# Eleven output products beside the last subtiles, folding of queries beside stage 2's products, and stage 2's bias on VectorE

## The chip, the cores and the metric

The kernel runs on one core of a Trainium2 chip. That core has five engines that run side by side: TensorE (PE in the profile; PEld is its weight load), VectorE (DVE), ScalarE (ACT), GpSimd (POOL) and SyncE (SP, which here only issues transfers). They share the on-chip memory SBUF; TensorE writes into the eight banks of PSUM, from which VectorE and ScalarE read. Transfers to and from the chip's main memory run on 16 DMA engines, and are issued from the queues of SP, ACT and POOL. Each engine works through its own instructions in a fixed order. The metric is device time in microseconds (us) from one launch.

## The reference

All is float32. Two cross-attentions follow each other over 4 x 1024 tokens of width 1024, each with a context of 64 rows per batch:

```python
# layer 0: 32 query heads of 32, 8 key/value heads
q, k, v = x @ Wq + bq, ctx @ Wk + bk, ctx @ Wv + bv
attn = softmax(q k^T / sqrt(32) + mask)           # per head, over 64 keys
h = (attn v) @ Wo + bo + x
x = layernorm(h, eps 1e-6) * gamma + beta
# layer 1: 16 heads of 64
a = layernorm(ctx) ; Q, K, V = x @ Wq.T, a @ Wk.T, a @ Wv.T
out = softmax(Q K^T / 8, masked) V @ Wo.T
y = x + tanh(gate) * out
```

## The kernel before, in words

Tokens come in 32 subtiles of 128 (t = 0 to 31), four blocks of eight, or 16 pairs. Large products are done in blocks of a two by two split, with seven products of blocks in place of eight (`products`, seven steps named X, V and W after the PSUM bank that each sums in). One step is four matmuls of 128 x 128 by 128 x 512, which the trace shows as eight records of L446, and one add of the bank to the row tile on VectorE (L455). The left operand's sums (`left_out`, L429 to L432) and the right operand's (`right_sums`, L183 to L186) are VectorE's too.

Stage 1 computes queries (L576) and layer 0's attention. For each subtile `mix` emits: two fronts (`front`, TensorE's scores L680 and VectorE's mask add L684), maxima (L691), subtraction of the maxima (L694), exponentials on ScalarE (whole in L706, or for `alone` heads one by one with their sum, L698), sums (L711), division (L715), then a transpose of the probabilities (`flip`; from subtile 19 on by TensorE, L407, with copies L410 or L414), the product with the values (`values`, L759) and a store of the result (L765). Between these, `other()` draws steps from one generator, `other_work`: the queries of later blocks, then the folding of layer 1's query weights into the keys, then the first steps of the output product of pair 0.

Folding of queries (`folded_queries`, eight chunks of four steps) multiplies K transposed by a chunk of Wq: per step four matmuls of 64 rows by 256 columns (L897, eight records), two evictions on ScalarE (L903), and after every second step a store of 1 MB on POOL's queue (L909). It also loads a chunk of wq1T on SP (L884). Eight steps go ahead of subtile 24 (`FOLD_AHEAD`), the other 24 and the first four product steps (`FIRST`) are shared out over the last eight subtiles. The weight wo is loaded in 16 parts on SP (L147).

Stage 2 is the output product: after the last three steps of pair 0, pairs 1 to 15 go through `project`, seven products with L455's adds, and between them steps of `fill`: the closing of the pair before (layer norm, L292 to L309, and its store L1053) and, for pairs 1 to 8, the folding of values into wo1 (`folded_values`, two steps `keys` of matmuls L924, evictions L929 and stores on SP L933). Rows of x come on SP (L954); the bias bo is added to them ahead of time on GpSimd (L958), for pair 0 on VectorE afterwards (L1095). Stage 3 is layer 1's attention with the folded weights. PSUM has four single banks (`wx`) and two double ones (`big`).

The kernel is written with a planner. It takes the program's order as priority and plans each engine's order from modelled times: an instruction whose inputs are ready in the model can go ahead of one that waits. `keep_in_program_order` exempts an instruction from that. Buffers come from pools with a number of slots per tag (`wpool`, tag "wb", has seven); a tile whose slot is in use waits for its release.

Of the kernel before, what the change touches and what calls it, by code (L numbers as in the profile page):

```python
# [19 lines left out]
B = 4  # L20
# [51 lines left out]
def tile_two_cross_attentions(  # L72
# [27 lines left out]
    def sub_ap(t):  # L100
        return slice(t * P, (t + 1) * P)
# [6 lines left out]
    ps_wx = ctx.enter_context(tc.tile_pool(name="ps_wx", bufs=4, space=bass.MemoryType.PSUM))  # L108
    ps_big = ctx.enter_context(tc.tile_pool(name="ps_big", bufs=2, space=bass.MemoryType.PSUM))

# [6 lines left out]
    def wx():  # L117
        return ps_wx.tile([P, 512], F32, tag="wx", name="wx")

# [21 lines left out]
    def block_of(w, i, j, tag, name, turned=False):  # L141
        t = new_block(tag, name)
        cols = slice(j * HW, (j + 1) * HW)
        if turned == "heads":
            rows = w.rearrange("(c g i e d) o -> c i e d g o", c=2, g=4, i=2, e=2)
            for a in range(NQ):
                nc.sync.dma_start(  # L147
                    out=t[a * Q : (a + 1) * Q], in_=rows[a // 2, a % 2, i][:, :, cols]
                )
        elif turned:  # L150
            rows = w.rearrange("(a k j) o -> a j k o", a=NQ, j=Q)
            for a in range(NQ):
                nc.sync.dma_start(
                    out=t[a * Q : (a + 1) * Q], in_=rows[a, :, i * HK : (i + 1) * HK, cols]
                )
        else:
            nc.sync.dma_start(
                out=t, in_=w[i * HW : (i + 1) * HW, cols].rearrange("(k p) o -> p k o", p=P)
            )
        return t  # L160
# [274 lines left out]
    def products(a, w, r, bias=None, tail=None):  # L435
# [6 lines left out]
        def product(name, s, m, first, last):  # L442
            if first:
                banks[name] = wx()
            for k in range(HK):
                nc.tensor.matmul(  # L446
                    banks[name], a[s][:, k, :], w[m][:, k, :],
                    start=first and k == 0, stop=last and k == HK - 1, skip_group_check=True,
                )
# [28 lines left out]
        ]  # L478
        return [lambda o=o: step(*o) for o in order]

    def project(a, w, r, fill, bias=None, tail=None):

        share = -(-len(fill) // 7)
        for step in products(a, w, r, bias, tail):
            step()
            for _ in range(min(share, len(fill))):
                fill.pop(0)()
# [150 lines left out]
    def by_turning(t):  # L638


        return t < NSUB - SUB - 5
# [12 lines left out]
    def attend0(t):  # L654
# [13 lines left out]
        alone = BY_HEAD if by_turning(t) else (4, 0) if t >= NSUB - SUB else (0, 0)  # L668
# [218 lines left out]
    def folded_queries(kT, wT, k):  # L887
# [3 lines left out]
        def heads(cc):  # L891
            banks = [wx(), wx()]
# [47 lines left out]
    def load_o(pair, pool, tag="o2"):  # L940
        o = pool.tile([P, KC, 2 * P], F32, tag=tag, name=f"o2_{pair}")
        load = nc.sync.dma_start(out=o, in_=oTd[pair])
        if pair < 2:
            tc.keep_in_program_order(load)
        return o

    def load_outputs(pair):
        o = load_o(pair, o2pool) if pair > 1 else second if pair else load_o(0, early)
        r = []
        for u in range(2):  # L950
            t = pair * 2 + u
            ru = (rpool.tile([P, H], F32, tag="r", name=f"r_{t}") if pair
                  else early.tile([P, H], F32, tag="r", name=f"r_{t}", bufs=2))
            load = nc.sync.dma_start(out=ru, in_=x[sub_ap(t), :])  # L954
            if not pair:
                tc.keep_in_program_order(load)
            if pair:
                nc.gpsimd.tensor_tensor(ru, ru, bo_sb, ALU.add)  # L958
            r.append(ru)
        return o, r  # L960

    def other_work(rows):

        nonlocal fold, early, bo_sb, w_o, first, first_rows, second
# [12 lines left out]
        queries_cm.close()  # L977
        fold = open_pool(fold_cm, "fold", 1)

        early = open_pool(early_cm, "early", 1)  # L980
        kT = fold.tile([P, KC, B * S], F32, tag="kvT", name="kT")
        nc.sync.dma_start(out=kT, in_=kTd)
        wT = turned_chunk(0)
        w_o, w_o_loads = right_loads(wo0, "wa", "wo0", "heads")
        bo_sb = constant(bo0.partition_broadcast(P), [P, H], "bo", F32, fold)
        for k in range(KC):
            ahead = turned_chunk(k + 1) if k + 1 < KC else None
            for step in folded_queries(kT, wT, k):
                step()
                yield  # L990
            wT = ahead
            if k in (1, 2, 3, 4):
                w_o_loads[k - 1]()
            if k == 5:
                run(right_sums(w_o))
                o, first_rows = load_outputs(0)
                a = left_out(o, early, "0_0")
        second = load_o(1, wpool, "wb")

        def tail():  # L1000
            nonlocal ahead_a
            ahead_a = left_out(second, early, "0_1")


        first = products(a, w_o, first_rows, None, tail)
        for _ in range(FIRST):
            first.pop(0)()
            yield

    fold_cm, early_cm = ExitStack(), ExitStack()  # L1010
    fold = early = bo_sb = w_o = first = first_rows = second = ahead_a = ahead_r = None
    FIRST = 4
# [3 lines left out]
    AHEAD, FOLD_AHEAD = 4, 8  # L1016
# [11 lines left out]
    n = 4 * KC - FOLD_AHEAD + FIRST  # L1028
    for i in range(SUB):
        mix(last + i, (i + 1) * n // SUB - i * n // SUB)  # L1030
# [17 lines left out]
    vT = fold.tile([P, KC, B * S], F32, tag="kvT", name="vT")  # L1048
# [20 lines left out]
    def turn_x1(pair, xq, pool=None, tag="xT"):  # L1069
# [15 lines left out]
    first.pop(0)()  # L1085
    flip(0)
    flip(1)
    first.pop(0)()
    values()
    open_stage()  # L1090
    _, ahead_r = load_outputs(1)
    run(first)

    fill = [
        lambda u=u: nc.vector.tensor_tensor(first_rows[u], first_rows[u], bo_sb, ALU.add) for u in range(2)  # L1095
    ]
    fill += close_rows(0, first_rows)
    for pair in range(1, NPAIR):
        r, a = ahead_r, ahead_a
        if pair + 1 < NPAIR:  # L1100
            ahead_o, ahead_r = load_outputs(pair + 1)
        if pair <= KC:
            ahead_w = chunk(wo1, pair, "wo1") if pair < KC else None
            fill += folded_values(vT, wch, pair - 1)
            wch = ahead_w
        if pair == KC + 2:
            w_a, w_a_sums = right_weight(ad[0], "wb", "a0", True)
        if pair in (NPAIR - 3, NPAIR - 2):
            fill += w_a_sums[0:2] if pair == NPAIR - 3 else w_a_sums[2:4]
        if pair == 3:  # L1110
            early_cm.close()
            xTpool = open_pool(last_cm, "x1T", 1)
            lxpool = open_pool(last_cm, "leftx", 1)
            xqpool = open_pool(last_cm, "x1q", 1)
        if pair == NPAIR - 4:
            xq = load_x1(1)
# [10 lines left out]
        project(a, w_o, r, fill, tail=tail)  # L1127
        fill = close_rows(pair, r)
# [112 lines left out]
    fold_cm.close()  # L1241

# [54 lines left out]
```

## Time and profile before

| | |
|---|---|
| Median of 3 runs | 1914.9 us (1913.46 to 1915.07) |
| The profiled execution | 1915.11 us, of which the span of its instructions is 1913.3 us |
| TensorE / VectorE / ScalarE / GpSimd busy | 1868.9 / 1292.1 / 427.9 / 179.1 us |
| Mean granted TensorE clock | 0.995 |
| Last subtiles (24 to 31), VectorE from its first to its last part | 598.9 to 705.4 us |
| Stage 2, pairs 1 to 15 | from about 720 to 1130 us |
| GpSimd's bias adds (L958) | 30, 2625 ns each |

A row of a timeline or chain reads: start, duration, engine and line, operation, out<-in by the program's names, shapes and a count; in brackets the idle time of the engine before it and what ended it. A row of windows gives for each engine its busy time in the window and the number of instructions, then TensorE's granted clock, the mean busy share of the DMA engines, and GB/s. A busy TensorE may still run below its peak, since matmuls are pipelined and the clock can be throttled.

### The profile page before, as it was taken

Reading aid. Unit: us, or ns where it says so; the run is one execution under the profiler, and the core shown is the slowest. Engines: PE = TensorE matmul, PEld = TensorE weight load, DVE = VectorE, ACT = ScalarE, POOL = GpSimd, SP = SyncE. Lnnn points to the kernel's source line nnn. Section 1 sums busy time; section 2 is a strip of 40 time slices with the busy share of each in tenths; the row PEclk is TensorE's granted clock in tenths of the full one; section 3 lists DMA queues with packets and bytes.
Section 4 is the critical chain, followed back from the end, with each engine's and each line's share of the span. In section 5 each row is a group of like instructions: output and inputs, shape, how many; then the busy total and the mean of one; then the engine's idle time right before and its main releaser. Section 6 shows DMA issues by size and latency. Waiting matters only on the chain.

```text
span 1913.3 us, 17522 instructions
## 1 busy us (share of the span) xinstructions
PE 1868.9 (98%) x6096; PEld 880.0 (46%) x6096; DVE 1292.1 (68%) x1582; ACT 427.9 (22%) x1396; POOL 179.1 (9%) x212
## 2 busy tenths in 40 slices
PE   8999999999998899999999999999999999999999
PEld 7744444444455653343344444444444444444444
DVE  3425589789878985575568778557665766576653
ACT  1101575666536751212100001000000000000000
POOL 0016011111100103121113100000000000000000
PEclk9999999999999899999999999999999999999999
DMA  8996599899878966567473363466656565657421
GB/s 276 184 222 192 158 253 247 253 252 261 252 186 275 302 234 207 188 207 238 164 218 138 121 141 90 110 165 158 150 143 165 150 158 143 165 142 165 121 88 44
DMA packets 220745, 350.54 MB, mean 183 GB/s; under 512 B 26992, under 2 KB 146160, under 8 KB 215664
## 3 DMA queue, kind: packets, MB, share of 16 engines
q1 hardware_dynamic: 152896, 242.44, 45.8%
q0 software_dynamic: 15216, 60.83, 10.5%
q10 hardware_dynamic: 52544, 46.14, 8.8%
q8 instruction: 48, 0.79, 0.2%
q14 instruction: 41, 0.34, 0.1%
HBM read 207.53 MB, written 141.82 MB: 183 GB/s over the span
## 4 chain that ended last, share of the span: by engine, by line
PE 82%; DVE 8%; DMA 5%; issue 2%; ACT 2%; POOL 0%; SPq 0%; DVEq 0%; POOLq 0%; ACTq 0%
PE wx L446 59%; PE wx L576 14%; PE big L680 2%; DMA pq<-p 2%; PE big L924 1%; PE wx L379 1%; PE big L379 1%; DVE s L684 1%; PE big L759 1%; DMA p<-s 1%; DMA q<-qTd 1%; DVE s L715 1%; DVE mx L691 1%; DVE sm L711 1%; DMA o<-oTd 1%
## 5 line engine op out<-in xcount | busy, mean ns | idle before, releaser
L455 DVE TENSOR_TENSOR r<-wx,r 128x512 f32<-128x512 f32 x224 | 153.5, 686 | 230.1 <-PE wx L446 215.3
L698 ACT ACTIVATE s<-s,mx 128x64 f32<-128x64 f32 x488 | 162.8, 335 | 74.9 <-DVE mx L691 70.7
L502 ACT ACTIVATE s<-s 128x1024 f32<-128x1024 f32 x32 | 33.7, 1057 | 651.7 <-DVE s L501 651.7
L459 DVE TENSOR_TENSOR s<-wx,key_bias 128x512 f32<-128x512 f32 x64 | 44.1, 690 | 136.7 <-PE wx L446 136.7
L446 PE MATMUL wx<-wo_B,S 128*128 128x512 f32 x256 | 117.1, 600 | 1.5 <-DVE r L455 1.5
L576 PE MATMUL wx<-xT,wq_S 128*128 128x512 f32 x256 | 116.5, 598 | 0.8 <-ACT z L587 0.8
L446 PE MATMUL wx<-b_B,pT 128*128 128x512 f32 x256 | 115.8, 593 | 0.6 <-ACT pT L414 0.6
L446 PE MATMUL wx<-b_B,S_p 128*128 128x512 f32 x256 | 116.0, 596 | 0.0
L446 PE MATMUL wx<-a_B,xT 128*128 128x512 f32 x256 | 115.4, 592 | 0.0
L446 PE MATMUL wx<-a_B,S_x 128*128 128x512 f32 x256 | 115.3, 593 | 0.1
L576 PE MATMUL wx<-xB,wq_A 128*128 128x512 f32 x256 | 115.1, 597 | 0.0
L446 PE MATMUL wx<-wo_B,o 128*128 128x512 f32 x256 | 114.8, 596 | 0.0
L958 POOL TENSOR_TENSOR r<-r,bo 128x1024 f32<-128x1024 f32 x30 | 78.5, 2625 | 313.8 <-DMA r<-in_x_dram 159.4
L684 DVE TENSOR_TENSOR s<-big,m 128x1024 f32<-128x1024 f32 x64 | 77.4, 1215 | 28.4 <-PE big L680 26.8
L680 PEld LDWEIGHTS big<-kv,q 64*128 64x128 f32 x1024 | 71.1, 195 | 48.3 <-issue 39.9
L698 ACT ACTIVATION_READ_ACCUMULATOR s<-s,mx 128x1 f32 x488 | 91.4, 187 | 0.0
L680 PE MATMUL big<-kv,q 64*128 64x128 f32 x1024 | 82.6, 292 | 2.6 <-DMA q<-qTd 2.6
L419 DVE STREAM_TRANSPOSE pT<-pq 128x1024 f32<-128x1024 f32 x66 | 78.0, 1219 | 3.3 <-DMA pq<-p 3.3
L446 PEld LDWEIGHTS wx<-wo_B,S 128*128 128x128 f32 x256 | 47.1, 190 | 67.7 <-issue 51.2
L715 DVE TENSOR_TENSOR s<-s,sm 128x1024 f32<-128x1024 f32 x64 | 77.0, 1216 | 0.9
L446 PEld LDWEIGHTS wx<-wo_B,o 128*128 128x128 f32 x256 | 47.8, 190 | 63.5 <-issue 62.3
L446 PEld LDWEIGHTS wx<-a_B,S_x 128*128 128x128 f32 x256 | 48.5, 190 | 62.0 <-issue 58.4
(162 smaller groups left out, 2903.5 us busy)
## 6 DMA issues: line engine op xcount, KB each, us to landing
p<-s POOLq DMA_DIRECT2D x19, 1024.0 KB, 8.1
pq<-p POOLq DMA_DIRECT2D x76, 256.0 KB, 6.0
xq<-in_x_dram SPq DMA_DIRECT2D x64, 256.0 KB, 10.2
q<-qTd SPq DMA_DIRECT2D x32, 512.0 KB, 7.4
oTd<-oT ACTq DMA_DIRECT2D x32, 512.0 KB, 7.4
ad<-a POOLq DMA_DIRECT2D x16, 1024.0 KB, 8.9
o<-oTd SPq DMA_DIRECT2D x16, 1024.0 KB, 5.1
r<-in_x_dram SPq DMA_DIRECT2D x32, 512.0 KB, 5.3
```

The lines of the kernel that those rows point to most:

```text
L379: nc.tensor.matmul(ps[:, 0:256], w[k // HK, c // HK][:, k % HK, sub_ap(c % HK)], ct[:, k, :], start=(k == 0), stop=(k == KC - 1),)
L419: return nc.vector.transpose(dst.rearrange("p k (u i) -> p k u i", i=Q), t[:, :, k0 * Q : k1 * Q].rearrange("p u (k j) -> p k u j", j=Q),)
L446: nc.tensor.matmul(banks[name], a[s][:, k, :], w[m][:, k, :], start=first and k == 0, stop=last and k == HK - 1, skip_group_check=True,)
L455: nc.vector.tensor_tensor(at, bank, at, ALU.add)
L459: nc.vector.tensor_tensor(at, bank.rearrange("p (h s) -> p h s", s=S), bias.unsqueeze(1).to_broadcast([P, 512 // S, S]), ALU.add,)
L502: nc.scalar.activation(s, s, AF.Exp)
L576: nc.tensor.matmul(bank, w_q[a][:, k, sub_ap(i)], rows[b][:, k, :], start=first and k == 0, stop=last and k == HK - 1, skip_group_check=True,)
L680: nc.tensor.matmul(ps[:, at : at + P], q[on, c * 4 + g, :], k0bd[on, b, c, :], start=True, stop=True,)
L684: nc.vector.tensor_tensor(quarters[:, :, c * 8 : (c + 1) * 8], ps.rearrange("p (k a l) -> p a k l", a=NQ, l=Q), mask.rearrange("p e (h l) ...
L698: nc.scalar.activation(heads[:, e, k], heads[:, e, k], AF.Exp, bias=mx[:, e, k : k + 1], accum_out=sm[:, e, k : k + 1],)
L715: nc.vector.tensor_tensor(heads[:, e], heads[:, e], wide(sm[:, e]), ALU.mult)
L958: nc.gpsimd.tensor_tensor(ru, ru, bo_sb, ALU.add)
```

## The change

Of the output product, pairs 0 and 1 but for pair 1's last three steps now stand beside subtiles 26 to 31: eleven steps, in an order that finishes bank X first, so that one PSUM bank (`sum_bank`) serves all of them. `share_banks` splits the four single banks into three and this one for that stretch. Only three of eight chunks of folded queries stay ahead of and beside subtiles 24 and 25 (four steps ahead, four in each); their wo sums are popped between them. The other five chunks stand between the products of stage 2's pairs 3 to 7 (after products 0, 2, 3 and 5), evicted from the double banks, and the folding of values moves to pairs 3 to 10, after products 1 and 4. Stage 2's loop starts at pair 2, whose fill closes pairs 0 and 1. All bias adds are made by VectorE as part of the closing. In the last eight subtiles 8 and 4 heads of the two halves, not 4 and 0, are exponentiated one by one on ScalarE. The parts of wo are loaded from POOL's queue, all before the folding, not from SP's. Rows of pairs 0 and 1 and the inputs of pairs 0 to 2 are loaded into slots of `wpool`.

```diff
+    def share_banks(name, sums):
+        nonlocal ps_wx, ps_sum
+        ps_cm.close()
+        ps_wx = ps_cm.enter_context(
+            tc.tile_pool(name=f"ps_wx{name}", bufs=4 - sums, space=bass.MemoryType.PSUM, reuse_waits="tile")
+        )
+        ps_sum = sums and ps_cm.enter_context(
+            tc.tile_pool(name=f"ps_sum{name}", bufs=sums, space=bass.MemoryType.PSUM, reuse_waits="tile")
+        )
+    share_banks("0", 0)
...
+    def sum_bank():
+        return ps_sum.tile([P, 512], F32, tag="sum", name="sum") if ps_sum else wx()
...
             for a in range(NQ):
-                nc.sync.dma_start(
+                nc.gpsimd.dma_start(
                     out=t[a * Q : (a + 1) * Q], in_=rows[a // 2, a % 2, i][:, :, cols]
                 )
...
             if first:
-                banks[name] = wx()
+                banks[name] = sum_bank()
...
+        if one_bank:
+            order = [order[i] for i in (0, 1, 3, 4, 2, 5, 6)]
         return [lambda o=o: step(*o) for o in order]
-    def project(a, w, r, fill, bias=None, tail=None):
+    def project(a, w, r, fill, bias=None, tail=None, beside={}):
         share = -(-len(fill) // 7)
-        for step in products(a, w, r, bias, tail):
+        for i, step in enumerate(products(a, w, r, bias, tail)):
             step()
+            if i in beside:
+                beside[i]()
...
-        alone = BY_HEAD if by_turning(t) else (4, 0) if t >= NSUB - SUB else (0, 0)
+        alone = BY_HEAD if by_turning(t) else (8, 4) if t >= NSUB - SUB else (0, 0)
...
-            banks = [wx(), wx()]
+            banks = two() if pairs else [wx(), wx()]
...
-            if pair:
-                nc.gpsimd.tensor_tensor(ru, ru, bo_sb, ALU.add)
...
+        share_banks("1", 1)
...
         w_o, w_o_loads = right_loads(wo0, "wa", "wo0", "heads")
+        run(w_o_loads)
+        sums = right_sums(w_o)
         bo_sb = constant(bo0.partition_broadcast(P), [P, H], "bo", F32, fold)
-        for k in range(KC):
-            ahead = turned_chunk(k + 1) if k + 1 < KC else None
-            for step in folded_queries(kT, wT, k):
+        for k in range(FOLDED):
+            ahead = turned_chunk(k + 1) if k + 1 < FOLDED else None
+            for n, step in enumerate(folded_queries(kT, wT, k)):
                 step()
+                if k > 0 and n % 2 and sums:
+                    sums.pop(0)()
                 yield
             wT = ahead
-            if k in (1, 2, 3, 4):
-                w_o_loads[k - 1]()
...
+        for pair in range(BESIDE):
+            o = load_o(pair, wpool, "wb")
+            rows = load_rows(pair)
+            if not pair:
                 a = left_out(o, early, "0_0")
...
+        for step in products(a, w_o, first[0][1], None, tail, True):
+            step()
             yield
+        for step in products(ahead_a[0], w_o, first[1][1], None, tail1, True):
+            steps.append(step)
+        while len(steps) > LEFT:
+            steps.pop(0)()
+            yield
+        rest.extend(steps)
...
+    FOLDED = 3
+    BESIDE = 2
+    LEFT = 3
-    AHEAD, FOLD_AHEAD = 4, 8
+    AHEAD, FOLD_AHEAD = 4, 4
...
-    n = 4 * KC - FOLD_AHEAD + FIRST
+    counts = [4, 4] + [(i + 1) * (7 * BESIDE - LEFT) // 6 - i * (7 * BESIDE - LEFT) // 6 for i in range(6)]
     for i in range(SUB):
-        mix(last + i, (i + 1) * n // SUB - i * n // SUB)
+        mix(last + i, counts[i])
...
+    share_banks("2", 0)
+    wT = turned_chunk(FOLDED)
+    def close_with_bias(pair, r):
+        return [
+            lambda u=u: nc.vector.tensor_tensor(r[u], r[u], bo_sb, ALU.add) for u in range(2)
+        ] + close_rows(pair, r)
+    fill = close_with_bias(0, first[0][1]) + close_with_bias(1, first[1][1])
+    FROM = BESIDE + 1
-    for pair in range(1, NPAIR):
+    for pair in range(BESIDE, NPAIR):
...
+        beside = {}
+        k = pair - FROM + FOLDED
+        if pair >= FROM and k < KC:
+            ahead_w = turned_chunk(k + 1) if k + 1 < KC else None
+            beside.update(zip((0, 2, 3, 5), folded_queries(kT, wT, k, True)))
+            wT = ahead_w
+        k = pair - FROM
+        if 0 <= k < KC:
+            ahead_w = chunk(wo1, k + 1, "wo1") if k + 1 < KC else None
+            beside.update(zip((1, 4), folded_values(vT, wch, k)))
             wch = ahead_w
...
-        project(a, w_o, r, fill, tail=tail)
-        fill = close_rows(pair, r)
+        project(a, w_o, r, fill, tail=tail, beside=beside)
+        fill = close_with_bias(pair, r)
```

## The prediction

> **What bounds the kernel now.** I read the page first (shares, slices), then busy times by windows around the last subtiles, then the chain of waits there, then the timelines of TensorE and VectorE in stage 2.
>
> ```profile
> PE 1868.9 (98%) x6096; PEld 880.0 (46%) x6096; DVE 1292.1 (68%) x1582; ACT 427.9 (22%) x1396; POOL 179.1 (9%) x212
> ```
>
> TensorE is called busy for 98%, so time is to be had only where it is slack or throttled. The windows (columns: busy us of each engine, granted clock, DMA share, GB/s) show where. The first row is subtiles 24 and 25, the next two 26 to 30, the fourth subtile 31, the last stage 2.
>
> ```profile
> 598.90:627.15 28.25, 22.49 (x199) 17.36 (x201) 22.76 (x24) 19.07 (x45) 3.01 (x4) 0.94 1.02 361
> 627.15:639.07 11.92, 11.22 (x109) 8.56 (x105) 11.34 (x14) 10.12 (x25) 1.51 (x2) 1.00 0.94 312
> 639.07:691.09 52.02, 44.65 (x345) 32.52 (x344) 48.02 (x54) 37.66 (x90) 5.27 (x7) 0.87 0.96 314
> 691.09:705.40 14.31, 14.07 (x72) 7.07 (x71) 13.12 (x16) 6.25 (x16) 0.00 (x0) 1.00 0.35 131
> 706.00:1130.00 424.00, 417.61 (x1027) 173.46 (x1026) 274.84 (x396) 49.31 (x101) 78.52 (x30) 1.00 0.56 179
> ```
>
> In the last subtiles VectorE sets the pace (11.34 of 11.92 us); the DMA engines are full, and TensorE loses clock and idles. In stage 2 TensorE is the bound and VectorE has a third of its time free. The chain shows one long wait in the first window: the queries of subtile 25 take 18.16 us to land, behind the folding's writes, against a median of 7.4 us.
>
> ```profile
> 593.45 18.16 DMA q<-qTd
> 611.74 1.40 PE big L680 x16
> ```
>
> In stage 2 (TensorE) one plain pair and the groups around an inserted folding of values read:
>
> ```profile
> 736.01 3.70 PE L446 MATMUL wx<-wo_B,S 128*128 128x512 f32 x8
> 739.64 1.98 PE L924 MATMUL big<-wo,vT 64*128 64x512 f32 x6
> 741.55 3.70 PE L446 MATMUL wx<-wo_N,o 128*128 128x512 f32 x8
> ...
> 804.61 1.99 PE L924 MATMUL big<-wo,vT 64*128 64x512 f32 x8
> 807.10 2.28 PE L924 MATMUL big<-wo,vT 64*128 64x512 f32 x8 [0.51 <-ACT b L929]
> ...
> 833.99 1.99 PE L924 MATMUL big<-wo,vT 64*128 64x512 f32 x8
> ...
> 1084.44 1.02 PE L446 MATMUL wx<-wo_T,o 128*128 128x512 f32 x2
> 1108.92 1.02 PE L446 MATMUL wx<-wo_T,o 128*128 128x512 f32 x2
> ```
>
> A plain pair takes 1108.92 - 1084.44 = 24.5 us, a pair with folding of values 833.99 - 804.61 = 29.4.
>
> **The change, part by part.** The sum goes against the profiled execution, 1915.1 us (span 1913.3 and 1.8 around it); the median of the runs, 1914.9, is 0.2 lower.
>
> *Stage 2.* (a) Pair 1 moves ahead but for three products, which take the place of pair 0's three: 15 pairs become 14, -24.5 us. (b) Twenty steps of folding queries come in. Eight steps standing alone took 8.03 us (62 records), so 1.0 each; an insertion costs 0.2 more, since a product group that leads into one takes 3.63 (739.64 - 736.01) against 3.43 (1094.99 - 1091.56). 20 x 1.24 = +24.8. Bounds: 20 x 1.0 = 20, and 20 x 2.1 = 42 if each cost what a folding step of values does (1.91 and 0.2); I take 1.24, as it is the same matmul. ScalarE's two evictions per step (610 ns each) lie beside a product. (c) The two folding steps of values in a pair stood together and waited for ScalarE (0.51 above): 4.9 us per pair over a plain one. Now a product stands between them: 2 x 2.1 = 4.2. Seven pairs, -4.9; nothing if the planner puts them together again. (d) GpSimd's 30 bias adds go (2.6 us each, 78.5). Pairs 11 to 13 took 25.0, 25.2 and 25.4 (wo_T,S groups at 1009.91, 1034.90, 1060.07, 1085.45) where an add of VectorE was caught by GpSimd, 2.1 over plain, and pair 1 waited 1.0 for a row not yet biased (725.31): -3.1. Bounds 0 and -3.1. (e) VectorE gets 30 x 1.226 = 36.8 us instead. Its two-input operations run slower beside GpSimd: L309 takes 1.27 alone and 3.18 beside it. The means over stage 2 (1466, 1540, 987, 960 and 928 ns against 1270, 1280 and 685 clear) make 5.9 + 7.8 + 4.5 + 4.1 + 3.6 = 26 us that come back. Net +11 in 424 us with 149 free: nothing, except at two places. (f) Pair 2 closes pairs 0 and 1 together, 28 steps instead of 16. Its VectorE work is two biases 2.5 and one more pair's (2.5, perhaps done earlier), four rows at 4.2, seven adds at 0.6 and the left sums 2.5: 26 to 28 us in a pair of 24.5, while beta, issued at 727.35, lands near 731.7 and shifts are due from about 728. An add behind them holds a bank, and TensorE waits. Bounds 0 (backlog carried into pair 3) and +7; I take +3. (g) The last pair's closing is 2.5 us longer where VectorE is dense (1126 to 1141, no gaps) and the first scores wait for its adds: 0 to +2.5, taken +1.5. Sum of stage 2: -24.5 + 24.8 - 4.9 - 3.1 + 3 + 1.5 = -3.2.
>
> *Last subtiles.* Eleven products and eight folding steps stand where four products and 24 steps did; four steps, not eight, go ahead of subtile 24. TensorE's filler there goes from 24 x 1.0 + 4 x 3.43 = 38 to 8 + 37.7 = 46 us. VectorE's work is 7 x 0.6 for adds and one left sum of 2.5 more. With eight and four heads by ScalarE, two subtractions and two sums shrink (948 + 1218 to 676 + 948, 951 + 1214 to 672 + 951): -1.08 per subtile, -8.7. Net -2 us. ScalarE gets eight heads more per subtile at 0.335 (four take 630.79 to 632.13) less 0.4 of whole exponentials: +2.3, and loses 16 steps' evictions. But VectorE's sum now waits for ScalarE to finish copies (1.5), the shorter whole exponential (0.85) and four heads (1.34) after the second maximum. In the window 627.15 to 639.07 that wait was 0.55; laid out with the new lengths the sum starts 1.5 later and the subtile lasts about 13.0. TensorE alone comes to 2 x 3.43 + 2.2 + 2.0 + 1.1 (fronts, transposes, values) and six switches of 0.2: 13.3. I take 13.35 for subtiles 26 to 31: 80.1 against 691.09 - 627.15 + 14.31 = 78.2: +1.9. Bounds: 12.6, VectorE's work alone (75.6, -2.6), and 15.0, subtile 31 as it is with 0.7 for waits on the one sum bank (+11.8). Subtiles 24 and 25 lose the flood ahead of q (two 1 MB writes early, not four): 2 x 13.0 = 26.1 against 28.25, -2.1; bounds 0 (q just as late) and -4.5 (11.9 each). Sum -0.2.
>
> *Queues.* The 16 loads of wo leave SP for GpSimd's queue, which issues nothing from 527.6 to 593.0, at 0.55 each: covered; were they late, the right sums would move from 585 to 598 into the subtiles, +9 at most, but they wait for the same w_q buffers as before, so 0. Rows and inputs of pairs 0 to 2 (5 MB) go on SP where fold traffic of 12.5 MB leaves; the DMA share there falls. Stage 2 takes up that 12.5 MB over five pairs of about 34 us: from 0.65 to about 0.75 of the DMA engines, with loads one pair ahead: 0. The closings' square roots stand behind ScalarE's evictions, which are 1.1 us per step in 4.7: 0.
>
> **Two rules that speak against the change.** Rows first: an insertion with its two changes of mode costs 0.2 us (3.63 against 3.43), and the clock was 0.87 in subtiles 26 to 30 with folding as filler, 1.00 in subtile 31 with products. I take 0.2 and 1.00. The Trainium skill, TensorEngine Tiling (Array Packing), Key Properties, says that a change of tiling mode drains TensorE; by its page TensorE: Matmul & The Clock Gate, Single matmul latency, a drain is some 0.17 us, so that 40 of them would, as an estimate, make 6.8 us in place of 4.0 and the sum 2.8 higher. The latter page, A second HAM failure mode, also says that cycling through PSUM banks lets TensorE idle and the clock fall; if the one sum bank kept it at half speed for a quarter of the 80 us, the estimate would be 10 us more.
>
> The sum is 1915.1 - 3.2 - 0.2 = 1911.7, less 0.2 for the median: **1911.5 us**, 0.18% below. 0.2% (3.8 us) is about what a measurement tells from no change.
>
> **The rivals.**
> *Slower: TensorE's queue binds subtiles 26 to 31.* One sum bank makes each product wait for VectorE's add of the one before, and the instruction behind it on TensorE waits too: a front, so VectorE starves. At 15.0 per subtile the window grows by 11.8: 1911.5 + 9.9 = 1921. It decides (over 0.2% slower) from 7.2 / 6 = 1.2 us per subtile over my 13.35. For it: subtile 31 took 14.31 with three products. Against: that was with a third more filler.
> *Faster: the subtiles shrink to VectorE's work.* 12.6 and 11.9 per subtile (-7.1), pair 2 and the tail without loss: -7.1 - 7.7 = 1900. For it: the add fits the new gap before the sums. Against: three engines above 85% each in one loop.
> *The swap gives nothing.* If the planner keeps foldings together (c = 0) and pair 2 costs 7: 1911.5 + 4.9 + 4 = 1920, or either alone 1915.5 to 1916.5: the same as before.
>
> **How the numbers follow.** Forecast 0.40, spread 1906 to 1917: faster 0.22, same 0.14, slower 0.04. Slower rival 0.28, all slower. Faster rival 0.20, all faster. Nothing gained 0.12: same 0.06, slower 0.06. Together faster 0.42, same 0.20, slower 0.38. The range cuts a tenth at each end, inside the outer rivals' bounds: 1899 to 1924; the forecast's own is 1906 to 1917.
>
> **What would show it.** The plain pair stays 24.5; a pair with both foldings takes 24.5 + 4.2 + 5.0 = 33.7 (above 36: b is wrong). L309 falls to 1.28 in the mean. q of subtile 25 lands within 12 us. Subtiles 26 to 31 last 79 to 82 us at clock 1.0. Pair 2 takes 27 to 28. The prediction is wrong if the subtiles pass 86 or fall below 76, or if ScalarE, short of a staging buffer for folding, delays the square roots and with them VectorE.

## The result, and the profile after

The changed kernel takes 1928.8 us (median of four runs, 1925.65 to 1929.24) against 1914.2 (1913.14 to 1915.07) for the kernel before: ratio 1.0072, 95% interval 1.0057 to 1.0087. It is slower by 14.6 us, where I forecast 3.4 us faster. The profiled execution is 1929.2 us long (span 1927.4). The page's row of busy times, after:

```profile
PE 1881.3 (98%) x6096; PEld 874.5 (45%) x6096; DVE 1294.7 (67%) x1612; ACT 449.5 (23%) x1526; POOL 109.3 (6%) x198
```

GpSimd lost its bias adds (179.1 to 109.3), TensorE's busy time grew by 12.4 for the same 6096 instructions. Where that lies is read from a few marks in the timelines: VectorE's first maximum of a subtile (L691 before, L712 after), the second product of the pair that opens stage 2 (pair 1 before, pair 2 after), and the first scores of stage 3.

| us | before | after |
|---|---|---|
| first maximum of subtile 24 | 602.34 | 604.69 |
| subtile 24 to 25 | 15.28 | 13.51 |
| 25 to 26 | 11.91 | **19.66** |
| 26 to 31 | 64.54 | 69.82 |
| 31 to the second product of stage 2's first pair | 29.25 | 26.58 |
| from there to the first scores | 406.64 | 409.86 |

The differences add to 14.2 us. The first, 2.35, is not the change's as far as the runs show: in the profiles of the experiments that build on the changed kernel (e, f, h1 and h3 below) this maximum stands at 600.62 to 603.10. The windows from maximum to maximum of subtiles 25 to 31, after (columns: busy us of each engine, clock, DMA share, GB/s):

```profile
618.20:637.86 19.66, 16.05 (x96) 9.79 (x96) 13.77 (x17) 11.03 (x39) 1.50 (x2) 0.91 1.03 367
637.86:650.31 12.45, 11.53 (x74) 5.97 (x72) 12.42 (x18) 8.04 (x32) 0.00 (x0) 1.00 0.91 302
650.31:665.21 14.90, 14.70 (x83) 7.55 (x82) 14.26 (x20) 8.21 (x32) 0.00 (x0) 1.00 0.53 156
665.21:679.90 14.69, 14.18 (x82) 7.28 (x81) 12.91 (x16) 8.30 (x32) 0.00 (x0) 1.00 0.27 74
```

The first has a hole: 19.66 us with 13.8 of VectorE's work, the DMA engines full. From the second on the clock is at 1.00, as forecast, and TensorE and VectorE are both nearly full. The chain of waits in the hole:

```profile
619.46 0.61 ACT s L719 x3
620.07 11.65 DMA o<-oTd
631.71 0.14 issue
631.85 5.38 PE sum L462 x8
```

The first product beside the subtiles needs pair 0's outputs, whose load goes out at 620.07 and takes 11.65 us. VectorE stands idle for 2.28 us at the left sums and for 1.89 us at the add of this product, and in its order both come ahead of subtile 26's maximum:

```profile
631.74 0.69 DVE L445 TENSOR_TENSOR S<-o 128x512 f32<-128x512 f32 x1 [2.28 <-DMA o<-oTd]
637.25 0.69 DVE L471 TENSOR_TENSOR r<-sum,r 128x512 f32<-128x512 f32 x1 [1.89 <-PE sum L462]
```

TensorE waits 2.56 us for the same load. Its eight records then take 5.37 us, not 3.70, at a granted clock of 0.69 (631.85 to 637.30):

```profile
631.85 5.37 PE L462 MATMUL sum<-wo_B,o 128*128 128x512 f32 x8 [2.56 <-DMA o<-oTd]
```

In stage 2 a second hole stands at the start of pair 13. TensorE, after:

```profile
1059.62 5.31 PE L462 MATMUL wx<-wo_B,o 128*128 128x512 f32 x12
1073.48 2.07 PE L462 MATMUL wx<-wo_T,o 128*128 128x512 f32 x2 [8.56 <-DVE o L447]
1075.35 4.36 PE L462 MATMUL wx<-wo_T,S 128*128 128x512 f32 x8
```

And VectorE in the same stretch:

```profile
1058.89 2.24 DVE L200 TENSOR_TENSOR a_T<-a_B,a_B 128x2048 f32<-128x2048 f32 x1
...
1064.16 2.35 DVE L1136 TENSOR_TENSOR r<-r,bo 128x1024 f32<-128x1024 f32 x2
1066.43 0.68 DVE L308 BATCH_NORM_STATS2 st<-r 128x6 f32<-128x512 f32 x1
1067.03 2.27 DVE L201 TENSOR_TENSOR a_T<-a_T,a_B 128x2048 f32<-128x2048 f32 x1
1069.22 2.28 DVE L202 TENSOR_TENSOR a_N<-a_B,a_T 128x2048 f32<-128x2048 f32 x1
1071.42 0.68 DVE L445 TENSOR_TENSOR S<-o 128x512 f32<-128x512 f32 x1
```

Three of the right sums of stage 3's first weight (w_a, wanted only at 1144) and two bias adds stand ahead of the left sums that pair 13 needs at 1065. The same three ran at 1017 to 1030 before, in pair 11:

```profile
1017.09 3.24 DVE L184 TENSOR_TENSOR a_T<-a_B,a_B 128x2048 f32<-128x2048 f32 x1
1020.37 2.29 DVE L185 TENSOR_TENSOR a_T<-a_T,a_B 128x2048 f32<-128x2048 f32 x1
1028.45 2.28 DVE L186 TENSOR_TENSOR a_N<-a_B,a_T 128x2048 f32<-128x2048 f32 x1
```

The folding of values now ends two pairs later, and the program loads w_a in pair 11 and not in pair 10 (`if pair == FROM + KC` in place of `if pair == KC + 2`): SP issues these loads from 1003.06 on, 965.51 before. Third, a pair that folds values alone (pairs 8 to 10), TensorE after:

```profile
923.97 1.12 PE L945 MATMUL big<-wo,vT 64*128 64x512 f32 x2
925.02 3.70 PE L462 MATMUL wx<-wo_T,S 128*128 128x512 f32 x8
928.65 1.98 PE L945 MATMUL big<-wo,vT 64*128 64x512 f32 x6
930.56 3.70 PE L462 MATMUL wx<-wo_T,o 128*128 128x512 f32 x8
934.10 3.60 PE L462 MATMUL wx<-wo_B,S 128*128 128x512 f32 x8
937.63 1.12 PE L945 MATMUL big<-wo,vT 64*128 64x512 f32 x2
938.68 3.70 PE L462 MATMUL wx<-wo_B,S 128*128 128x512 f32 x8
942.31 1.98 PE L945 MATMUL big<-wo,vT 64*128 64x512 f32 x6
```

Each step of eight records is split by the planner into two and six, which cost 1.05 and 1.91 us from start to start, where a whole one (in pairs 3 to 7) costs 1.92: the pair takes 30.75 (the group wo_B,o starts at 947.76 and at 978.51), against 29.4 before and the 28.7 that I forecast.

### The profile page after: what moved, and what is told of

Same layout as the page of the kernel before. It is cut to its first block, busy times and chain, and to the rows that moved or that the text cites. A ratio compares the mean times of both kernels' runs of the same rounds, so it can differ in the third digit from the quotient of the medians.

```text
span 1927.4 us, 17644 instructions
## 1 busy us (share of the span) xinstructions
PE 1881.3 (98%) x6096; PEld 874.5 (45%) x6096; DVE 1294.7 (67%) x1612; ACT 449.5 (23%) x1526; POOL 109.3 (6%) x198
## 4 chain that ended last, share of the span: by engine, by line
PE 83%; DVE 8%; DMA 4%; ACT 2%; issue 2%; POOL 1%; SPq 0%; DVEq 0%; POOLq 0%; ACTq 0%
PE wx L462 57%; PE wx L597 13%; PE big L701 2%; PE big L945 2%; PE sum L462 2%; PE wx L395 1%; PE big L395 1%; PE big L780 1%; DVE s L705 1%; PE big L918 1%; DMA p<-s 1%; DVE s L736 1%; DMA pq<-p 1%; DVE mx L712 1%; ACT s L719 1%
## 5 line engine op out<-in xcount | busy, mean ns | idle before, releaser
L471 DVE TENSOR_TENSOR r<-wx,r 128x512 f32<-128x512 f32 x210 | 143.9, 685 | 224.8 <-PE wx L462 224.6
L719 ACT ACTIVATE s<-s,mx 128x64 f32<-128x64 f32 x552 | 184.3, 336 | 84.3 <-DVE mx L712 80.2
L523 ACT ACTIVATE s<-s 128x1024 f32<-128x1024 f32 x32 | 33.7, 1057 | 651.8 <-DVE s L522 651.8
L719 ACT ACTIVATION_READ_ACCUMULATOR s<-s,mx 128x1 f32 x552 | 104.2, 189 | 0.0
L462 PE MATMUL wx<-wo_B,S 128*128 128x512 f32 x224 | 102.5, 600 | 0.4 <-DVE r L471 0.4
L462 PE MATMUL wx<-wo_B,o 128*128 128x512 f32 x224 | 99.2, 595 | 0.0
L701 PEld LDWEIGHTS big<-kv,q 64*128 64x128 f32 x1024 | 66.2, 189 | 50.4 <-issue 42.0
L462 PEld LDWEIGHTS wx<-a_B,xT 128*128 128x128 f32 x256 | 48.6, 190 | 61.2 <-issue 60.5
L462 PEld LDWEIGHTS wx<-b_B,S_p 128*128 128x128 f32 x256 | 47.6, 190 | 63.3 <-issue 51.6
L462 PEld LDWEIGHTS wx<-b_B,pT 128*128 128x128 f32 x256 | 48.5, 190 | 61.3 <-issue 60.0
```

Of the source, the lines that this page charges most:

```text
L462: nc.tensor.matmul(banks[name], a[s][:, k, :], w[m][:, k, :], start=first and k == 0, stop=last and k == HK - 1, skip_group_check=True,)
L471: nc.vector.tensor_tensor(at, bank, at, ALU.add)
L523: nc.scalar.activation(s, s, AF.Exp)
L701: nc.tensor.matmul(ps[:, at : at + P], q[on, c * 4 + g, :], k0bd[on, b, c, :], start=True, stop=True,)
L719: nc.scalar.activation(heads[:, e, k], heads[:, e, k], AF.Exp, bias=mx[:, e, k : k + 1], accum_out=sm[:, e, k : k + 1],)
```

## The experiments

Theories: (A) the order of VectorE's work in pairs 12 and 13 costs some 10 us; (B) the late load makes the hole at subtile 26; (C) ScalarE's heads make the later subtiles long. Rivals: the bias adds as such, the one sum bank, the wo loads' queue. All medians with the ratio to runs of the kernel before beside them (these have medians of 1913.4 to 1914.7, so that between runs of different groups the ratios are the better measure):

| run | median us | ratio (95%) |
|---|---|---|
| changed kernel | 1928.8 | 1.0072 (1.0057 to 1.0087) |
| e1 w_a's sums late | 1918.4 | 1.0019 (1.0010 to 1.0027) |
| e2 outputs early | 1929.9 | 1.0077 (1.0065 to 1.0089) |
| e3 bias on GpSimd | 1936.4 | 1.0112 (1.0099 to 1.0125) |
| e4 four heads | 1926.5 | 1.0056 (1.0042 to 1.0069) |
| f1 e1, outputs early, left sums in place | 1913.9 | 1.0000 (0.9990 to 1.0010) |
| f2 e1, keys in fill | 1914.7 | 1.0002 (0.9993 to 1.0011) |
| f3 e1, wo on SP | 1919.9 | 1.0031 (1.0019 to 1.0043) |
| f8 e1, two sum banks | 1921.9 | 1.0041 (1.0029 to 1.0053) |
| h1 e1, f1 and f2 together | **1911.3** | **0.9979 (0.9969 to 0.9989)** |
| h3 h1 with four heads | 1916.6 | 1.0009 (1.0001 to 1.0017) |
| h2 before, bias on VectorE | 1919.1 | 1.0020 (1.0011 to 1.0028) |
| h4 before, eight and four heads | 1926.4 | 1.0052 (1.0036 to 1.0068) |
| k1 h2, w_a's sums late | 1915.1 | 1.0008 (0.9999 to 1.0017) |
| k2 before, w_a's sums late | 1915.6 | 1.0011 (1.0002 to 1.0020) |

**e1: the order on VectorE.** `right_sums` gets a flag that pins each of w_a's sums behind the instruction before it in the program:

```diff
+        def tt(*a):
+            t = nc.vector.tensor_tensor(*a)
+            if fixed:
+                tc.keep_in_program_order(t)
...
-            w_a, w_a_sums = right_weight(ad[0], "wb", "a0", True)
+            w_a, w_a_sums = right_weight(ad[0], "wb", "a0", True, True)
```

> The changed kernel (1928.8 us, 14.6 above before) with one edit: the four sums of the next stage's first weight (w_a) keep their place in the program, in pairs 13 and 14, instead of being planned ahead in pairs 12 and 13. Theory A, that these sums stand on VectorE ahead of the left sums that pair 13's first product needs: VectorE reaches the left sums 6.8 us earlier (2.24 + 2.27 + 2.28), the wait of 8.56 us falls to about 2 and the drop of the clock after it goes; a sum of 2.3 us comes into pair 13 instead and may cost up to 2. 1920 to 1923. Rival, that the bias adds make VectorE too full in every pair: the work is the same, the wait only moves to pair 14: 1927 to 1930.

Measured 1918.4, 10.4 below. TensorE at the start of pair 13:

```profile
1063.77 1.12 PE L466 MATMUL wx<-wo_T,o 128*128 128x512 f32 x2 [1.73 <-DVE o L451]
```

The wait is 1.73 instead of 8.56, and the records behind it run at full pace (1.12 for two, not 2.07). From the second product of pair 2 to the first scores the kernel takes 402.2 us, 7.7 less; the other 2.7 of the median lie outside the edit (this profile is 3.2 ahead at subtile 24 already), so 8 to 10 us is what A is worth. A holds.

**e2: the load earlier.** The loads of pair 0's outputs and rows go ahead of the third folded chunk:

```diff
         for k in range(FOLDED):
+            if k == FOLDED - 1:
+                loaded = load_o(0, wpool, "wb"), load_rows(0)
...
-            o = load_o(pair, wpool, "wb")
-            rows = load_rows(pair)
+            o, rows = (load_o(pair, wpool, "wb"), load_rows(pair)) if pair else loaded
```

> The changed kernel with one edit: the first pair's outputs and rows are loaded one folded chunk earlier (ahead of the third chunk), so that the load stands ahead of the queries of subtile 27 on SP and not behind them. Theory B, that the gap of 19.7 us between the maxima of subtiles 25 and 26 (11.9 in before) is the wait for this load, 11.65 us after an issue at 620.07: the load goes out by 610 and lands by 622, the gap falls to about 13 and the time by 5 to 7: 1922 to 1924. Rival, that the gap is made by the queries or by the product's place on TensorE's queue: unchanged within 1.5 us, and later q of subtile 27 a new wait.

Measured 1929.9, no gain. VectorE in this run:

```profile
617.55 0.69 DVE L445 TENSOR_TENSOR S<-o 128x512 f32<-128x512 f32 x1 [3.27 <-DMA o<-oTd]
...
619.49 1.22 DVE L705 TENSOR_TENSOR s<-big,m 128x1024 f32<-128x1024 f32 x1
```

The load went out at 605.44 and took 12.09 us. But the planner moved the left sums one subtile forward too, now ahead of subtile 25's second mask add: the gaps became 18.6 (24 to 25) and 16.1 (25 to 26), 34.7 together against 33.2. The hole itself is mended, then (16.1 for 19.7, and f1 below has 16.0), and the gap before it has grown. How far the left sums did that is not shown: TensorE's granted clock was 0.72 in that gap (1.00 in the changed kernel), and the front that the mask add needs ended only at 618.7, 0.8 us ahead of the mask add:

```profile
618.45 0.27 PE L701 MATMUL big<-kv,q 64*128 64x128 f32 x1
```

In pair 2 TensorE then waits 2.54 us for an add of VectorE (0.44 in the changed kernel). So by the medians the early load alone gains nothing, and this one profile does not show whether that is the left sums' doing.

**f1: the load earlier and the left sums in their place**, on top of e1:

```diff
-        nc.vector.tensor_tensor(s["S1"], a21, a22, ALU.add)
+        first = nc.vector.tensor_tensor(s["S1"], a21, a22, ALU.add)
+        if pool is early:
+            tc.keep_in_program_order(first)
```

> The kernel with w_a's sums late (1918.4 us), and two edits in the last subtiles: the first pair's outputs are loaded one folded chunk earlier, and the first of each pair's left sums keeps its place in the program, so that VectorE does not stand waiting for the load ahead of its mask adds. Theory B, that the gap of 19.4 us between the maxima of subtiles 25 and 26 is VectorE (and TensorE behind it) waiting for the load: the load is issued near 606 and lands by 618, the left sums come up after 620 and wait for nothing, the gap falls to 13.5 to 14.5: -5 to -6, 1912.5 to 1914. Rival, that the transfers of that stretch (DMA share 1.0) are the limit and the wait only moves to the queries of subtile 27 or 28: 0 to -2, 1916.5 to 1918.5.

Measured 1913.9, 4.5 below e1, in the range of B. VectorE at the left sums, which now wait for nothing:

```profile
622.66 1.22 DVE L711 TENSOR_TENSOR s<-big,m 128x1024 f32<-128x1024 f32 x1
623.80 0.68 DVE L449 TENSOR_TENSOR S<-o 128x512 f32<-128x512 f32 x1
624.39 0.68 DVE L738 TENSOR_REDUCE sm<-s 128x8 f32<-128x512 f32 x1
```

25 to 26 takes 15.98 (19.45 in e1), 26 to 31 takes 68.0 (69.8). B holds in this form: the late load made the hole. Pinning the left sums without the earlier load was not run, so how the gain divides between the two edits is not shown. A little over 2 us more than a plain subtile's time stays in the first gap; TensorE is busy for 15.43 us of it and the DMA share is 1.06.

**f2: keys among the closing steps again in pairs 8 to 10**, on top of e1:

```diff
-            beside.update(zip((1, 4), folded_values(vT, wch, k)))
+            if pair - FROM + FOLDED < KC:
+                beside.update(zip((1, 4), folded_values(vT, wch, k)))
+            else:
+                fill += folded_values(vT, wch, k)
```

> The kernel with w_a's sums late (1918.4 us), and one edit: in pairs 8 to 10, which fold values alone, the two folding steps are put among the closing steps as before, where the planner may set them together, and not one after the second and one after the fifth product. If setting them apart costs (30.75 us per pair against 29.4 in before): 3 x 1.35, -4, 1914 to 1915. If what I forecast for setting them apart holds and something else makes the pair long: 1918 to 1919.

Measured 1914.7, 3.7 below e1. TensorE in pair 8:

```profile
934.18 1.12 PE L949 MATMUL big<-wo,vT 64*128 64x512 f32 x2
935.24 3.70 PE L466 MATMUL wx<-wo_B,S 128*128 128x512 f32 x8
938.87 1.98 PE L949 MATMUL big<-wo,vT 64*128 64x512 f32 x6
940.78 3.70 PE L466 MATMUL wx<-wo_N,o 128*128 128x512 f32 x8
944.41 1.99 PE L949 MATMUL big<-wo,vT 64*128 64x512 f32 x8
```

One of two steps is split and not both; a pair takes 29.7 (928.08, 957.78, 987.48).

**f3: wo's loads on SP**, on top of e1:

```diff
-                nc.gpsimd.dma_start(
+                nc.sync.dma_start(
                     out=t[a * Q : (a + 1) * Q], in_=rows[a // 2, a % 2, i][:, :, cols]
```

> The kernel with w_a's sums late (1918.4 us), and one edit: the sixteen loads of wo are issued by SyncE again and not by GpSimd. If GpSimd's queue makes them late (its loads wait until 572, and wo's first sum runs at 569 in the full stretch of VectorE and not at 554 in a gap): the first mask add of subtile 24 comes 1.9 earlier, 1916 to 1917. If the queue is nothing to it, as I forecast: 1918 to 1919.

Measured 1919.9, not below e1. wo's first sum did move into the gap (552.31), but the mask adds that gained room then wait:

```profile
599.21 1.22 DVE L709 TENSOR_TENSOR s<-big,m 128x1024 f32<-128x1024 f32 x1 [1.95 <-PE big L705]
601.52 1.23 DVE L709 TENSOR_TENSOR s<-big,m 128x1024 f32<-128x1024 f32 x1 [1.08 <-PE big L705]
```

In e1 they stand at 599.12 and run through. The next releaser, TensorE's front, is later than VectorE was.

**f8: two sum banks**, on top of e1, which leaves two for copies, values and folding:

```diff
-        share_banks("1", 1)
+        share_banks("1", 2)
```

> The kernel with w_a's sums late (1918.4 us), and one edit: in the last subtiles the products have two banks for their sums and the copies, values and folding two in place of three. My slower rival, that the one bank makes subtiles 27 to 31 last 14.0 us in the mean and not 13.35: -0.5 to -0.7 each, -3, 1915 to 1916. If VectorE and TensorE are simply full (13.1 and 13.3 us busy of 14.0): 1918 to 1920, or more where two banks are too few for the copies.

Measured 1921.9, 3.5 above e1. 27 to 31 takes 56.4 (648.84 to 705.25), 57.4 in e1: 0.25 less per subtile, not 0.6. And pair 2 gives back more than that: VectorE, there earlier, waits 4.34 for beta, and TensorE behind it:

```profile
739.74 5.40 PE L466 MATMUL wx<-wo_B,S 128*128 128x512 f32 x8 [3.12 <-DVE r L475]
```

This run also takes a bank from the copies, the values and the folding, so it does not test the one bank alone. But the changed kernel's own trace does: from the maximum of 26 to that of 31 TensorE waits for the sum bank once, for 0.92 us. My slower rival, with 1.65 us per subtile for the one bank, falls.

**e4 and h3: four heads by ScalarE, not eight and four**, in the changed kernel and in the repaired one:

```diff
-        alone = BY_HEAD if by_turning(t) else (8, 4) if t >= NSUB - SUB else (0, 0)
+        alone = BY_HEAD if by_turning(t) else (4, 0) if t >= NSUB - SUB else (0, 0)
```

> The changed kernel with four heads of the first group by ScalarE in the last subtiles, as before, in place of eight and four. VectorE gets 1.08 us more per subtile, ScalarE 2.3 less. Theory C, that ScalarE's longer chain (eight and four heads ahead of the sums) makes subtiles 27 to 31 last 14.5 and not 13.35: they fall to 13.0 to 13.5, -5 to -7, 1922 to 1924. Rival, that the products and their adds on one sum bank make them long: VectorE's 1.08 comes on top, +5 to +8, 1934 to 1937.

> The kernel with the three edits and four heads of the first group by ScalarE in place of eight and four. If VectorE and ScalarE are both near the bound in subtiles 26 to 31, as the run of this edit alone showed (VectorE busy for all of 67.9 us, 1.9 less than with eight and four): 1909 to 1912, no difference from the three edits alone. If ScalarE's chain binds there: -3 or more, 1907 or less.

e4 measured 1926.5, between the two theories and not to be told from the changed kernel; h3 1916.6, 5.3 above h1. The windows of subtiles 26 to 28 in e4:

```profile
634.69:647.56 12.87, 11.11 (x85) 6.31 (x84) 12.87 (x15) 5.97 (x16) 0.00 (x0) 1.00 0.96 319
647.56:660.46 12.90, 12.26 (x71) 6.49 (x70) 12.90 (x16) 6.10 (x16) 0.00 (x0) 1.00 0.30 83
660.46:673.96 13.50, 13.20 (x76) 6.93 (x75) 13.50 (x17) 6.10 (x16) 0.00 (x0) 1.00 0.26 74
```

VectorE is busy for every microsecond: in these subtiles, with four heads, it is the bound. Five such subtiles took 67.9 us (69.8 in the changed kernel), but the 1.9 us and more were lost in pair 2, where the first shift waits 4.38 us for beta and TensorE 2.53 behind it. In h3 the five subtiles took 71.35 us, longer than with eight and four heads (68.04 in h1). C falls: ScalarE's heads are not what lengthened the subtiles. Neither range for h3 held, 1909 to 1912 or 1907 and less. That with the load repaired eight and four heads are 5 us better is measured, but only part of it is placed: in h3's profile pair 2 takes 1.8 more (27.5 by 25.7), and from the maximum of subtile 25 to pair 2 nothing is lost (111.0 by 110.6). The other 3.6 stand between subtiles 24 and 25 (17.2 by 13.5). There TensorE's granted clock was 0.70 in h3's profile and 1.00 in h1's. It was 0.70 in f2's as well (17.3 us, with eight and four heads) and 1.00 in e4's (13.0, with four), so the profiles do not tie that loss to the heads.

**h4: eight and four heads alone**, in the kernel before:

```diff
-        alone = BY_HEAD if by_turning(t) else (4, 0) if t >= NSUB - SUB else (0, 0)
+        alone = BY_HEAD if by_turning(t) else (8, 4) if t >= NSUB - SUB else (0, 0)
```

> The kernel before with one part of the change alone: eight and four heads by ScalarE in the last subtiles in place of four. VectorE gets 1.08 us less in each of eight subtiles of 11.9 us that it bounds (-8.7 if nothing else binds). By my layout of the chain its sum then starts 1.5 us later, so that a subtile lasts 0 to 0.6 longer: 1915 to 1919. If VectorE alone sets the pace: 1907 to 1910.

Measured 1926.4, 11.7 above before and beyond my range. The windows of subtiles 25 and 26:

```profile
616.36:629.79 13.43, 11.86 (x103) 8.93 (x102) 10.58 (x12) 13.09 (x43) 1.50 (x2) 1.00 1.00 316
629.79:642.23 12.44, 10.77 (x93) 7.83 (x92) 10.68 (x12) 11.57 (x40) 0.78 (x2) 1.00 0.80 268
```

ScalarE, which also evicts the folding there, is at 13.09 of 13.43 and 11.57 of 12.44: the same edit that does no harm beside products makes the six gaps from 25 to 31 last 83.9 us beside folding (76.5 before). That is not all of the 11.7: this profile, at 1920.2, is of the shortest of six executions, only 5.1 above that of before, and where the others lose the rest is not shown.

**e3, h2, k1, k2: who adds the bias.** e3 puts the adds of the changed kernel back on GpSimd (`nc.gpsimd.tensor_tensor` in `close_with_bias`), where they stay part of the closing and do not go ahead of it as in the kernel before; h2 moves them to VectorE in the kernel before; k1 is h2 with w_a's sums pinned, k2 the kernel before with only that:

```diff
-            if pair:
-                nc.gpsimd.tensor_tensor(ru, ru, bo_sb, ALU.add)
...
-        fill = close_rows(pair, r)
+        fill = close_with_bias(pair, r)
```

> The changed kernel with stage 2's 30 bias adds back on GpSimd (30 x 2.6 us). If the bias adds on VectorE make the wait ahead of pair 13's first product: it goes with the clock's drop, -10, 1919. If the order of the weight's sums makes it: 2.35 us of bias adds go from in front of the left sums, the wait falls from 8.6 to about 6, while VectorE's shift (L325) takes 3.18 again where it lies beside GpSimd and a late row makes a pair wait up to 1 or 2 us: 1926 to 1930.

> The kernel before with one part of the change alone: stage 2's 30 bias adds on VectorE. My terms (d) and (e): GpSimd's waits go in pairs 1 and 11 to 13, VectorE's 36.8 us are covered: -3.1, 1911. If the 10 us of the changed kernel's pair 13 come from the bias adds alone, they show here too: 1920 or more. Going back to GpSimd in the changed kernel cost 7.6 us, most of it where pair 2 closes two pairs; of that nothing is to be had here.

> The kernel before with the bias adds on VectorE (1919.1 us alone) and w_a's four sums kept in their place in pairs 13 and 14. If the place of the sums ahead of the left sums is what costs (pair 12 took 27.4 us and pair 13 28.5 against 24.5, with a wait of 3.17 and the clock at half): both pairs fall to about 24.5, -7, and what is left is my term (d): 1911 to 1913. If the adds' own 36.8 us are too much for VectorE: 1918 to 1920.

> The kernel before with w_a's four sums kept in their place in pairs 13 and 14 and nothing else. There is no wait for left sums in pairs 11 to 13 of before, so nothing is to be gained; the sums come into pairs with more work of VectorE: 1914 to 1917. If it gains 2 or more, the late place is better by itself, and the 10 us that it gained in the changed kernel are not all the change's.

e3 measured 1936.4, 7.6 above: neither theory. The hole in pair 13 stayed (9.88), since GpSimd beside VectorE made one of w_a's sums last 4.42 us and a scale 3.31, and two waits came in at pair 2 and right behind it:

```profile
738.14 3.70 PE L462 MATMUL wx<-wo_B,S 128*128 128x512 f32 x8 [1.04 <-DVE r L471]
...
758.97 5.40 PE L462 MATMUL wx<-wo_T,S 128*128 128x512 f32 x8 [2.15 <-DVE r L471]
```

TensorE's waits for VectorE in stage 2 come to 15.0 us, 9.0 in the changed kernel.

h2 measured 1919.1, 4.4 above before. It shows the same hole as the changed kernel, in pair 12, smaller:

```profile
1035.65 1.12 PE L446 MATMUL wx<-wo_T,o 128*128 128x512 f32 x2 [3.17 <-DVE o L431]
1037.98 6.43 PE L446 MATMUL wx<-wo_T,S 128*128 128x512 f32 x8 [1.21 <-DVE r L455]
```

Here too w_a's sums (three of 2.24 to 2.28 us) came ahead of the left sums once VectorE had the bias adds, and two pairs took 27.4 and 28.5 us. k1 measured 1915.1, 4.0 below h2 by the medians and 2.3 by the ratios: with the sums late the wait is 1.00. k2 measured 1915.6: the late place gains nothing by itself. So the bias adds on VectorE cost or gain nothing measurable (k1 against k2), and their price came through the planner's order.

**h1: the three repairs together.**

> The changed kernel with all three edits that gained: w_a's sums late, the first pair's outputs earlier with the left sums in their place, and pairs 8 to 10 with the keys' folding among the closing steps. If the three are separate places on the path, the gains add: 1928.8 - 10.4 - 4.5 - 3.7 = 1910.2, which would also be the sum of my prediction without these three. If they hide one another (a stall that waits in another's place): 1913 to 1915.

Measured 1911.3, 17.5 below the changed kernel and 0.21% below before. The gains of e1, f1 and f2 add, within the noise (18.6 by their medians, 17.0 by their ratios). From the first maximum of subtile 24 (603.10) to the second product of pair 2 it takes 124.1 us (129.6 in the changed kernel, 121.0 before), from there to the first scores 399.1 (409.9, 406.6). It beats both kernels. That it lies where the prediction put the change is in part luck: with three edits that the prediction did not have, stage 2 is 7.5 shorter than before, where 3.2 was forecast, and the last subtiles are 3.1 longer, where 0.2 less was forecast.

## Why the prediction was wrong, step by step

- **(a)** Right. A plain pair takes 24.42 (1016.12 to 1040.54), and there is one less.
- **(b)** Right. A pair with both foldings takes 33.31, four times the same (783.66, 816.97, 850.28, 883.59, 916.90); 33.7 was forecast.
- **(c)** Wrong for three of its pairs. "Now a product stands between them: 2 x 2.1" holds in pairs 3 to 7, within their 33.31, and fails in pairs 8 to 10: 30.75, not 28.7, +6.2 us. I had bounded it by "the planner puts them together again"; it took them further apart, two records and six, and each piece pays for itself. The trace of before had this: the row of six at 739.64, which the prediction shows, has its two at 734.95, in a pair that took 29.77 (725.31 to 755.08) and not 29.4. f2 gives back 3.7. The term also counts seven pairs where eight fold values.
- **(d)** The waits on GpSimd went (pairs without folding 24.4), but the 3.1 us did not come: alone (k1 against k2) there is no measurable gain, because a pair with values' folding then took 29.7 and not 29.4, and pair 12 waited 1.00.
- **(e) is the step that failed, and cost most.** The sizes were right: L325 fell to 1.28 us, as forecast, with no execution above 1.286, and VectorE has time in the sum. "Nothing, except at two places" left out a third: pair 13, with its hole of 8.56 us. I counted VectorE's free time over 424 us and did not ask in which order its work would stand there once w_a became ready later. That w_a's loads move from pair 10 to 11 was in the change, and no term of the sum had it. What the runs showed in its place: three of w_a's sums, 2.24 to 2.28 us each, ahead of the left sums that TensorE waits for; in their later place (e1) they give back 8 to 10.
- **(f)** Mechanism right, size off: beta came late (VectorE waited 3.64), TensorE only 0.44; pair 2 took 25.4, +1 instead of +3. **(g)** 0 instead of +1.5: the last stretch took 20.8 us (1123.32 to 1144.12), 21.0 before.
- **Last subtiles.** From the maximum of 24 to that of 25 this profile gains 1.8, and the queries of 25 no longer stand in the chain there; but in f2's and h3's profiles the same gap loses 2 at a lower clock, so a gain like the 2.1 forecast is not shown. Six subtiles at 13.35 were to take 80.1. The six gaps between maxima from 25 to 31 took 89.5 (76.5 before); by the prediction's own stretch, from 26's first mask add to 31's last division, it is 94.6 (625.85 to 720.41) against 78.2. Both are above the 86 that it named as a sign of being wrong. Of the 9.4 that the gaps have over 80.1, some 5 are the load (f1: 84.0), which is the **queue term**: "Rows and inputs of pairs 0 to 2 (5 MB) go on SP where fold traffic of 12.5 MB leaves; the DMA share there falls." It stood in the sum as nothing. The share fell only later (0.53, 0.27); where it counts it was 1.03, the load took 11.65 us, and it was issued 9.4 us before VectorE wanted it (620.07, idle from 629.46). I had weighed the wo loads, which are no better on SP (f3), and not the load that the first product waits for. The other 4 are 13.6 per subtile with a longer first one, against 13.35.
- **The rivals.** The slower one gave 1921, with a product that waits for its bank and a front that waits behind it. A product did wait, but for a DMA (2.56 us), and VectorE then waited for this product's sum and not for a front. For the bank TensorE waited 0.92 us in all.
- **The rules.** Rows first: 33.31 - 24.42 = 8.89 us for six steps, which alone last 4 x 1.0 + 2 x 1.91 = 7.8, leave 0.18 per insertion, as the 0.2 forecast. The clock was 1.00 in every subtile from the second product on. The Trainium skill's drain at a change of mode (TensorEngine Tiling (Array Packing), Key Properties) cannot have cost more than these 0.18 us for two changes, about half of what the prediction's estimate from the skill had. Its warning of cycling through PSUM banks (TensorE: Matmul & The Clock Gate, A second HAM failure mode) is not tested by a single sum bank.

## What to carry to other kernels

When work is moved, list for each engine what becomes ready later through it (here a weight's loads, which the program issues a pair later) and look which instruction will stand ahead of the one that the bound engine needs next; a sum of free time over a long stage does not show it. A load that becomes the operand of an inserted product has to be issued a whole loaded transfer time ahead, by the trace's own landing time in that stretch. Here that gained only together with a pin on its consumer (f1), since the planner had taken the consumer along (e2). Test each part of a change both alone and in its company: eight and four heads cost 11.7 us in the kernel before, made no clear difference in the changed one (e4) and were 5.3 better in the repaired one (h3).

## What the runs showed of the hardware

- After a wait of 8.56 us TensorE ran at a granted clock of 0.52 for the next 3.5 us: two records took 2.07 us instead of 1.02, and the pair behind it 25.8 us (1073.48 to 1099.29) instead of 24.4. In h2 waits of 3.17 and 1.21 were followed by a product of 6.43 instead of 3.70 (clock 0.57). In e3, e4 and f8 waits of 2.15, 2.53 and 3.12 were followed by one of 5.40 (0.67 to 0.68), in e2 one of 2.54 and in e1 one of 1.73 by none. A wait can cost twice.
- A gain ahead of pair 2 does not always arrive: in e4 and f8 VectorE came there earlier and waited 4.4 us for beta, whose load goes out some 10 us after gamma's.
- A step of eight 64-row records that is split into two and six costs 1.04 us more than whole (1.05 and 1.91 for 1.92, from start to start).
- VectorE's operations beside GpSimd's add are stretched: in e3 a sum of 2048 columns that alone takes 2.27 us took 4.42, in the kernel before one took 3.24.
